# A graph network with sorted neighbours: due times step by step, the order of loads, and three small edits around TensorE

## The chip, the cores and the metric

The kernel runs on one core of a Trainium2 chip. The metric is device time in microseconds (us). Five engines of the core matter here: PE (TensorE, the matrix engine), PEld (its weight loads, which overlap with matmuls), DVE (VectorE), ACT (ScalarE) and POOL (GpSimd); SP issues most of the DMAs. Each engine executes its instructions in the order in which the program gives them, and waits at an instruction whose inputs aren't there.

## The reference

There are 128 graphs of N = 128 nodes with F = 64 features, and a dense matrix `adj` (128 x 128) for each, about 6% of it non-zero. Two layers follow one another, each with a residual and a layer norm:

```
mask = adj > 0
h  = relu(x_j @ W1a + (x_j - x_k) @ W1b + b1)          # for each pair j, k; H = 192
hm = sum over k of mask[j, k] * h[j, k]
x  = layernorm(x + hm @ W2 + deg[j] * b2)              # deg = row sums of mask
agg = adj @ x
x  = layernorm(x + elu(elu(agg @ V1 + c1) @ V2 + c2) @ V3 + c3)
```

## The kernel before, in words

**Tiling.** Two graphs make a pair (index s), and there are NP = 64 pairs p. For a node j, the sum over k needs only its neighbours. The kernel therefore counts the degrees, sorts the nodes of each graph by degree (a rank by comparisons, then a permutation matrix), and gives each of the 9 column blocks of sorted nodes (BLOCKS) a fixed number of neighbour slots. For a block of w nodes with s slots, n = s*w columns; the nine n make E = 1323 columns a graph. A one-hot matrix `oh` (from a running count of the mask along the sorted nodes) picks the neighbour for each slot by a matmul, so that the sum over k becomes a sum over slots.

**One pair, step by step** (line numbers of the kernel before):

- `prepare` (L502): mask and degrees on DVE (L511), keys on POOL (L518), `spread` on PE (L524 spreads the degrees over the columns; L526 makes a row 0, 1/128, ... from the constants `small` and `iotb`), `rank` on DVE (L533), `permute` on DVE (L541: permutation matrix `permb`, comparing L526's row in PSUM with the ranks).
- `sort_x` (L548): the sorted x (L556), then `project_a` (L564): three f32 matmuls L570 and the bias on ACT (L577) make `aj`; POOL and DVE make a correction for unused slots (L584, L596, L603), with a small matmul step L589/L591.
- `sort_mask` (L606): L612, L615 on PE, copies on ACT (L620, L622), a running count L626, then nine one-hot blocks on DVE (L636).
- `turn` (L645): transposes of adj and x (L651, L652), one copy on ACT (L656).
- `project_c` (L661): the neighbours' half of the first product, for each of the two graphs one f32 matmul with 64 rows of contraction and 256 columns (L669; graph 0 uses rows 0 to 63 of the array, graph 1 rows 64 to 127), and a bias row (L672). Its 256 columns are 192 of the hidden layer and 64 of the product with W2. The result is split into three bf16 parts on ACT, DVE and POOL (L679, L683, L686, L688): `cp`.
- nine `unit`s (L803): ACT copies `aj` into one of NE = 4 PSUM banks (L811), 18 bf16 matmuls add the neighbours' parts (`gather`, L823; columns 0 to 63 and 64 to 127 of the array work as two tiles), DVE reduces over the slots (L832) into `sums`.
- `finish` (L736): `hm` on POOL (L741); `project` on PE (L746 with `hm`, L750 with the sorted mask and `cp`, L753 counts the slots from a column of ones); `ys` on ACT (L757), a store of the counts (L759), `unsort` (L763), a norm (L691: DVE, POOL, ACT), `aggregate` (L770), two hidden layers (L778/L780 and L786/L787, each with exp on ACT and a DVE step), `last` (L792/L794), a second norm and the store of the result.

After the loop, `dense` computes pairs whose degrees don't fit the slots in another way. With these inputs it only finds that there are none.

**What sets the order.** The class `Flow` (L63) is a planner that runs when the program is built. Every pair has several threads (generators); each yields its next step as (engine, cost, events it needs, PSUM banks it needs, function). `Flow.run` keeps a clock for each engine, finds for each thread when its step could start, takes the engine with the earliest, and among the steps that could start within NEAR of that the one with the smallest due time (`_rank`). A step that would change TensorE's tiling mode (`PE` or `PE:t`) ranks HOLD later and costs SWITCH more. The function then emits the instructions. So costs and due times decide only the order on each engine; the chip runs it with semaphores. Before, a thread has one due time at its start and moves by a fixed pace with each step (STEP = 1.94, or 0.1 for constants); pair p's preparation begins when pair p - AHEAD's gathers do, with AHEAD = 3 and ROUND = 11.39 a pair. `load` (L496) issues the DMAs of adj and x on SP; the planner takes them as there 2.5 after its latest clock.

Of the kernel before, what the change touches and what calls it, by code (L numbers as in the profile page):

```python
# [87 lines left out]
class Flow:  # L88
# [10 lines left out]
    NEAR = 0.1  # L99
    NEAR_PE = 0.05  # L100
    SWITCH = 0.1
    HOLD = 5
# [8 lines left out]
    def start(self, due, pace, gen):  # L111

        self.serial += 1
        th = [due, self.serial, pace, gen, None]
        self._next(th, None)

    def _next(self, th, got):
        try:
            th[4] = th[3].send(got)
        except StopIteration:  # L120
            if th in self.threads:
                self.threads.remove(th)
            return
        if th not in self.threads:
            self.threads.append(th)
        elif got is not None:
            th[0] += th[2]
# [50 lines left out]
def sparse(tc, env):  # L178
# [6 lines left out]
    NE = 4  # L185
# [7 lines left out]
    ROUND = 11.39  # L193
    AHEAD = 3
    PACE = ROUND / NB
    STEP = 1.94
    TURN = 4
    CS = 3
    SORT = 5
    FIN = 0.5  # L200

    def due(p, step):
        return ROUND * (p - AHEAD) + STEP * step

    def pace(u):
        return PACE * u

# [26 lines left out]

    def fetch(t, src):
        nc.sync.dma_start(t, src)
# [24 lines left out]
    wc = const([P, H + O], F32, "wc")  # L261
# [9 lines left out]
    b2p = const([P, O], BF16, "b2p")  # L271
# [35 lines left out]
    def arrive_next():  # L307
        halves(nc.sync, b1c, g.b1, [[1, HB], [HB, 3]])
        fetch(b2r, bass.AP(tensor=g.b2.tensor, offset=g.b2.offset, ap=[[0, P], [1, O]]))
        happened([6.0], "const", "b1")  # L310
        happened([6.0], "const", "b2")

    def arrive_late():
        fetch(v2s, g.v2)
        fetch(v3s, g.v3)
        for s in range(2):
            fetch(v1d[s * F:(s + 1) * F], g.v1)
        for c, lo, times in ((g.c1, 0, 1), (g.c2, H1, 1), (g.c3, 2 * H1, 2)):
            n = c.shape[0]
            fetch(rows[:, lo:lo + times * n].rearrange("p (t n) -> p t n", t=times),  # L320
                  bass.AP(tensor=c.tensor, offset=c.offset, ap=[[0, P], [0, times], [1, n]]))
        happened([14.0], "const", "v")
        happened([14.0], "const", "c")
# [12 lines left out]
    def consts_pool():  # L336
# [11 lines left out]
        flow.start(0.1, 0.1, consts_prefix(below))  # L348
        yield from op("POOL", 0.2, lambda: v.memset(b2p, 0.0), "b2p0")
# [8 lines left out]
        yield from op("POOL", 1.0, scale, "srow")  # L358
        for s in range(2):
            yield from op("POOL", 0.3, lambda: v.memset(v1p[:, s], 0.0), f"v1p0{s}")  # L360
# [9 lines left out]
    def consts_dve():  # L370
# [8 lines left out]
        yield from op("DVE", 0.4, lambda: v.memset(wad, 0.0), "wad0")  # L379

# [14 lines left out]
    def consts_w():  # L395

        v = nc.vector
        yield from op("DVE", 0.25, lambda: v.tensor_scalar(wc[:, 0:H], w1s[:, 1], -1.0, None,
# [15 lines left out]
        ev, = yield ("DVE", 0.2, [ev], 0, lambda: v.tensor_scalar(wc[:, H:H + O], t[:, :O], 0.5,  # L414
# [13 lines left out]
    def consts_b2():  # L428
        last = ["b2", "b2p0"]
        for name, fn in parts(b2r, b2p, O):  # L430
            yield from op("POOL", 0.25, lambda: fn(nc.gpsimd), "b2" + name, *last)
            last = ["b2" + name]
        happened(event("const", "b22"), "const", "b2p")
# [68 lines left out]
    def prepare(p):  # L502
# [19 lines left out]
        def spread(key):  # L522
            for s in range(2):
                nc.tensor.matmul(key[:, s * N:(s + 1) * N], degb[:, s:s + 1].to_broadcast([P, P]),  # L524
                                 identb, start=True, stop=True)
            nc.tensor.matmul(key[:, 2 * N:3 * N], small, iotb, start=True, stop=True)  # L526
        ev, key = yield ("PE", 0.17, [ev] + made("identb", "small", "iotb"), 1, spread)
# [8 lines left out]
        ev, = yield ("DVE", 0.54, [ev] + made("tie"), 0, rank)  # L536
        permb = d["permb"] = prep.tile([P, 2, N], BF16, name="permb")

        def permute():
            for s in range(2):  # L540
                nc.vector.tensor_scalar(permb[:, s, :], key[:, 2 * N:3 * N], pos[:, s:s + 1], None,  # L541
                                        op0=OP.is_equal)
        ev, = yield ("DVE", 0.51, [ev], 0, permute)
        flow.give(key, ev)
        flow.start(due(p, SORT), STEP, sort_x(p, ev))
        flow.start(due(p, SORT), STEP, sort_mask(p, ev))
# [98 lines left out]
    def turn(p):  # L645
# [13 lines left out]
        flow.start(due(p, CS), STEP, project_c(p, ev))  # L659

    def project_c(p, ev):  # L661

        d = S[p]
        cols = H + O

        def project(*cps):
            for s in range(2):
                k = slice(s * F, (s + 1) * F)
                nc.tensor.matmul(cps[s][:, :cols], d["turned"][k, 2, :], wc[k, :],  # L669
                                 start=True, stop=False)  # L670
            for s in range(2):
                nc.tensor.matmul(cps[s][:, H:cols], onesb[:, :P], b2p, start=False, stop=True)  # L672
        ev, *cps = yield ("PE", 0.7, [ev] + made("wc", "b2p", "onesb"), 2, project)
# [62 lines left out]
    def finish(p):  # L736
# [5 lines left out]

        def project(yb):
            cp, mtp = d["cp"], d["mtp"]
            for c in range(3):
                nc.tensor.matmul(yb[:, :2 * O], hm[:, c, :], flat(w2d[:, c]),  # L746
                                 start=(c == 0), stop=False)
            for s in range(2):
                for i in range(3):
                    nc.tensor.matmul(yb[:, s * O:(s + 1) * O], mtp[:, s, :], cp[:, i, s, H:H + O],  # L750
                                     start=False, stop=(s == 1 and i == 2))
            for s in range(2):
                nc.tensor.matmul(yb[:, 2 * O + s:2 * O + s + 1], mtp[:, s, :], onesb[:, 0:1],  # L753
                                 start=True, stop=True)
        ev, yb = yield ("PE", 0.9, [ev] + made("w2d"), 1, project)
        ys = work.tile([P, 2 * O + 2], F32, name="ys")
        ev, = yield ("ACT", act(2 * O + 2), [ev], 0, lambda: nc.scalar.copy(ys, yb[:, :2 * O + 2]))  # L757
        flow.give(yb, ev)
        nc.sync.dma_start(g.degs[:, 2 * p:2 * p + 2], ys[:, 2 * O:])  # L759

        def unsort(t):
            for s in range(2):
                nc.tensor.matmul(t[:, s * O:(s + 1) * O], d["permT"][:, s, :],  # L763
                                 ys[:, s * O:(s + 1) * O], start=True, stop=True)
# [74 lines left out]
    def begin(p):  # L839
        if p < NP:  # L840
            load(p)
            happened([max(flow.clock.values(), default=1.0 + p) + 2.5], "load", p)
            flow.start(due(p, 0), STEP, prepare(p))
            flow.start(due(p, TURN), STEP, turn(p))
# [3 lines left out]
    def lane(u, ev):  # L848
        p = units[u][0]
        if p not in begun:  # L850
            begun.add(p)
            begin(p + AHEAD)
            flow.start(ROUND * (p + FIN), STEP, finish(p))
        ev = yield from unit(u, ev)
        if u + NE < len(units):
            flow.start(pace(u + NE), PACE, lane(u + NE, ev))

    nc.vector.memset(mone, -1.0)
    for p in range(min(AHEAD, NP)):
        begin(p)  # L860
        if p == 0:
            arrive_next()
    arrive_late()
    flow.start(-101.0, 0.1, arrive())
    flow.start(-100.0, 0.1, consts_pool())
    flow.start(-99.0, 0.1, consts_dve())
    flow.start(-98.0, 0.1, consts_w())
    flow.start(-97.0, 0.1, consts_wad())
    flow.start(-96.0, 0.1, consts_b2())
    flow.start(-95.0, 0.1, consts_banks())  # L870
    flow.start(ROUND * -0.5, 1.0, consts_late())
    for k in range(NE):
        flow.start(pace(k), PACE, lane(k, [0.0]))
# [217 lines left out]
```

## Time and profile before

| what | before |
|---|---|
| median of 3 runs | 788.52 us (788.28 to 788.82) |
| the profiled execution | 789.11 us |
| its span, first to last instruction | 787.3 us |
| granted TensorE clock, mean | 0.991 |
| PE busy | 756.4 us (96%), 14551 matmuls |
| PEld busy | 684.9 us (87%) |
| DVE busy | 736.8 us (94%) |
| ACT busy | 661.6 us (84%) |
| POOL busy | 441.7 us (56%) |
| costliest group: gather matmuls L823 | 376.4 us, 10368 of them |

A page of the profile gives the busy time of each engine, the span in slices, the DMA queues, the chain of work that ended last, and groups of instructions (line, engine, operation, out<-in, count, busy us, mean ns, idle before it and what ended it). Matmuls are pipelined and their ends are modelled, so that their durations overlap; what a matmul takes of TensorE's time is read from the distance between starts. A timeline lists instructions in order of time, with equal neighbours merged: start, length from the first start to the last end, count. f32 matmuls appear as two records each.

### The profile page before, as it was taken

The page shows a single profiled execution, that of the slowest core. Times are in us where ns is not written, and L with a number is a line of the kernel's source. Part 1 is how long each engine was busy: PE and PEld are TensorE (multiplying, and loading weights), DVE is VectorE, ACT ScalarE, POOL GpSimd, SP SyncE. Part 2 cuts the span into 40 slices and gives each one's busy share as a digit, 9 for nine tenths or more (in the row PEclk, how much of TensorE's full clock was granted, in tenths as well). Part 3 has the DMA queues.
Part 4 walks back from the last instruction along what each step waited for, and adds up shares of the span by engine and source line. Part 5 has one row for each costly group of instructions (what it writes and reads, how often), then busy time and mean ns, then how long its engine had stood idle before and what let it go on. Part 6 is the DMA issues. An engine that isn't in the chain of part 4 may idle for free.

```text
span 787.3 us, 35836 instructions
## 1 busy us (share of the span) xinstructions
PE 756.4 (96%) x14551; PEld 684.9 (87%) x14552; DVE 736.8 (94%) x2421; ACT 661.6 (84%) x1862; POOL 441.7 (56%) x806
## 2 busy tenths in 40 slices
PE   4889999999999999999999999999999999999994
PEld 2578999999999999999999999999999999999983
DVE  3899999999999999999999999999999999999982
ACT  1868889898989989898998989889898988989862
POOL 4445556555655655565565556556556655655542
PEclk9999999999999999999999999999999999999996
DMA  3000101101101110110111011011101101110000
GB/s 95 2 2 23 27 22 27 30 20 30 26 20 30 27 29 20 30 27 20 30 27 29 21 30 26 20 30 26 30 20 31 26 20 30 27 28 21 9 9 14
DMA packets 63884, 19.91 MB, mean 25 GB/s; under 512 B 46560, under 2 KB 63712, under 8 KB 63712
## 3 DMA queue, kind: packets, MB, share of 16 engines
q1 hardware_dynamic: 63008, 17.25, 9.4%
q8 instruction: 116, 1.90, 1.0%
q14 instruction: 56, 0.46, 0.2%
q10 hardware_dynamic: 704, 0.30, 0.1%
HBM read 13.27 MB, written 4.19 MB: 22 GB/s over the span
## 4 chain that ended last, share of the span: by engine, by line
PE 91%; DVE 4%; ACT 1%; DMA 1%; issue 1%; SPq 1%; POOL 1%; ACTq 0%; POOLq 0%; DVEq 0%
PE e L823 43%; PE m L570 6%; PE m L746 6%; PE m L669 5%; PE m L780 4%; PE m L794 4%; PE m L787 4%; PE m L763 4%; PE m L770 2%; PE m L556 2%; PE m L651 2%; PE m L750 1%; PE m L672 1%; PE m L589 1%; DVE sums L832 1%; DVE oh L636 1%
## 5 line engine op out<-in xcount | busy, mean ns | idle before, releaser
L823 PE MATMUL e<-oh,cp 128*64 128x162 bf16 (+3 forms) x10368 | 376.4, 228 | 5.4 <-ACT e L811 3.8
L823 PEld LDWEIGHTS <-cp 128*64 128x64 bf16 x10368 | 349.1, 110 | 24.4 <-issue 16.9
L832 DVE TENSOR_REDUCE sums<-e 128x54 f32<-128x486 f32 (+8 forms) x576 | 345.6, 610 | 4.2 <-PE e L823 1.9
L811 ACT COPY e<-aj 128x504 f32<-128x504 f32 (+6 forms) x576 | 300.2, 549 | 17.0 <-DVE sums L832 11.6
L636 DVE TENSOR_TENSOR oh<-vp,slotc 128x336 bf16<-128x336 bf16 (+6 forms) x576 | 168.3, 321 | 0.7 <-PE e L823 0.5
L688 POOL TENSOR_TENSOR cp<-r,cp 128x512 bf16<-128x512 f32 x64 | 74.8, 1170 | 73.8 <-ACT cp L686 73.7
L709 POOL TENSOR_TENSOR rs<-ve,mhalf 128x2 f32<-128x2 f32 x128 | 89.2, 697 | 10.6
L577 ACT ACTIVATE aj<-m,b1c 128x128 f32<-128x128 f32 x192 | 56.5, 365 | 34.7 <-PE m L570 34.6
L741 POOL TENSOR_TENSOR hm<-sums,corr 128x384 f32<-128x384 f32 x64 | 64.3, 1004 | 31.1 <-DVE sums L832 31.1
L518 POOL CAST degb<-deg 128x2 bf16<-128x2 f32 x64 | 12.4, 193 | 122.5 <-DVE mk L511 122.5
L584 POOL TENSOR_TENSOR sa<-aj,srow 128x384 f32<-128x384 f32 x64 | 64.1, 1001 | 15.6 <-ACT xsT L560 8.3
L603 POOL TENSOR_TENSOR corr<-ea,sa 128x384 f32<-128x384 f32 x64 | 64.0, 1001 | 11.2 <-DVE ea L596 11.2
L679 ACT CAST cp<-m 128x256 bf16<-128x256 f32 x128 | 41.6, 376 | 33.3 <-PE m L672 33.2
L729 ACT ACTIVATE e<-m,mone 128x256 f32<-128x256 f32 x128 | 60.7, 474 | 6.7 <-PE m L787 3.7
L708 POOL TENSOR_SCALAR ve<-st 128x2 f32<-128x2 f32 x128 | 24.5, 191 | 67.1 <-DVE st L701 61.6
L732 DVE SCALAR_TENSOR_TENSOR h<-e,m 128x256 f32<-128x256 f32 x128 | 53.0, 414 | 5.5 <-ACT e L729 5.5
L570 PE MATMUL m<-xsT,wad 128*128 128x128 f32 x384 | 57.6, 287 | 0.5 <-DVE h L732 0.5
L746 PE MATMUL m<-w2d,hm 128*128 128x128 f32 x384 | 54.3, 278 | 0.0
L683 DVE TENSOR_TENSOR r<-m,cp 128x256 f32<-128x256 f32 x128 | 48.5, 419 | 5.8
L719 ACT ACTIVATE x<-y,nb,rs 128x64 f32<-128x64 f32 x128 | 51.1, 464 | 0.9 <-POOL nb L712 0.8
L570 PEld LDWEIGHTS m<-xsT,wad 128*128 128x128 f32 x384 | 48.7, 194 | 0.9 <-DVE h L732 0.7
L746 PEld LDWEIGHTS m<-w2d,hm 128*128 128x128 f32 x384 | 48.0, 192 | 1.1 <-POOL hm L741 0.2
(147 smaller groups left out, 1416.6 us busy)
## 6 DMA issues: line engine op xcount, KB each, us to landing
adj<-in_adj_dram SPq DMA_DIRECT2D x64, 128.0 KB, 2.4
xx<-in_x_dram SPq DMA_DIRECT2D x64, 64.0 KB, 2.1
out_dram<-o SPq DMA_DIRECT2D x64, 64.0 KB, 1.6
degs<-ys SPq DMA_DIRECT2D x64, 1.0 KB, 1.6
w1s<-in_L_gnn_W_dram ACTq DMA_DIRECT2D x2, 96.0 KB, 3.1
rows<-in_L_gnn_b_dram SPq DMA_DIRECT2D x3, 64.0 KB, 3.4
w2s<-in_L_gnn_W_dram ACTq DMA_DIRECT2D x2, 48.0 KB, 2.7
v2s<-in_L_gnn_W_dram SPq DMA_DIRECT2D x1, 64.0 KB, 2.3
```

What stands on the lines that cost most here:

```text
L570: nc.tensor.matmul(aps[:, c * N:(c + 1) * N], wad[:, c, :], xsT, start=True, stop=True)
L584: evs, = yield ("POOL PORT", 0.95, [have] + made("srow"), 0, lambda: nc.gpsimd.tensor_mul(sa, aj, srow))
L603: ev, = yield ("POOL PORT", 1.05, [ev, evs], 0, lambda: nc.gpsimd.tensor_sub(corr, ea, sa))
L636: lambda: nc.vector.tensor_tensor(oh[:, :, c].rearrange("p b (s w) -> p b s w", w=w), vp[:, :, p0:p1].rearrange("p b (o w) -> p b o w", o= ...
L688: lambda: nc.gpsimd.tensor_sub(cp[:, 2], r1, cp[:, 1]))
L709: nc.gpsimd.tensor_tensor(rs, ve, mhalf, op=OP.pow)
L729: lambda: nc.scalar.activation(e, z, AF.Exp, bias=mone))
L741: lambda: nc.gpsimd.tensor_sub(hm, d["sums"], d["corr"]))
L746: nc.tensor.matmul(yb[:, :2 * O], hm[:, c, :], flat(w2d[:, c]), start=(c == 0), stop=False)
L811: lambda: nc.scalar.copy(e.rearrange("p (c s w) -> p c s w", c=3, w=w), d["aj"][:, :, p0:p1].rearrange("p c (o w) -> p c o w", o=1) .to_br ...
L823: nc.tensor.matmul(e[s * HB:(s + 1) * HB, c * n:(c + 1) * n], cp[:, k, s, c * HB:(c + 1) * HB], oh[:, s, base:base + n], start=False, stop ...
L832: nc.vector.tensor_reduce(d["sums"][:, :, p0:p1], e.rearrange("p (c s w) -> p c w s", c=3, w=w), AX.X, OP.add, apply_absolute_value=True)
```

## The change

- **Due times.** Every step gets a due time of its own, from a table DUE (relative to 10.83 times the pair's number), in place of start plus pace. NEAR goes from 0.1 to 0.05, HOLD from 5 to 1.3, ROUND from 11.39 to 10.83, AHEAD from 3 to 4. `consts_pool`, `consts_dve` and `consts_b2` are partly put off.
- **Queue of loads.** The planner keeps a clock of SP's queue (`queued`), and `arrive_late`, which loads the second net's weights, is called after the loads of the first five pairs.
- **Counts from a column of ones.** `wc` and `b2p` get two columns more; the bias row writes ones into them. `cp` is then 258 wide, and its W2 part has a column of ones on either side. The L750 matmuls take 65 columns and give the counts with the product; the L753 matmuls go. The L750 matmuls stand ahead of those with `hm`.
- **Row tiles of C in turns.** L669's two matmuls of 256 columns become four of 129: first half of graph 0, of graph 1, second half of graph 0, of graph 1.
- **Permutation from a row in SBUF.** `permute` compares with `iotb` in SBUF (bf16, the rank as it is), and L526 goes.

```diff
-    NEAR = 0.1
+    NEAR = 0.05
-    HOLD = 5
+    HOLD = 1.3
...
-    def start(self, due, pace, gen):
+    def start(self, base, due, gen):
...
+        th[0] = th[5] + next(th[3], th[0] - th[5])
         if th not in self.threads:
             self.threads.append(th)
-        elif got is not None:
-            th[0] += th[2]
...
-    ROUND = 11.39
-    AHEAD = 3
+    ROUND = 10.83
+    AHEAD = 4
     PACE = ROUND / NB
-    STEP = 1.94
-    TURN = 4
-    CS = 3
-    SORT = 5
-    FIN = 0.5
...
+    DUE = {
+        "prepare": (-44.8, -59.6, -54.3, -49.4, -45.1),
+        "sort_x": (-26.9, -23.7, -23.1, -22.6, -17, -21.2, -16.5, -16.5, -21.8),
+        "sort_mask": (-21.1, -43.6, -19.4, -7.5, -12.1, -5.1, -3, -0.9, 0.5, 0.1, 0.5, 6.9, 7,
+                      11.5),
+        "turn": (-44.7, -37.6),
+        "project_c": (-29.2, -26.7, -30.6, -30.3, -23.4, -20.3, -25.3),
+        "finish": (27.2, 19.6, 18.9, 24.1, 25.9, 27.6, 31.3, 28.1, 22.5, 34.7, 38.1, 42.8, 40.5,
+                   44, 46.5, 46.7, 52.9, 53, 54.5, 58.2, 65.2),
+        "unit": (1.7, 26, 7.9),
+    }
...
+    SP = [0.7]
+
+    def queued(cost):
+
+        SP[0] = max(SP[0], max(flow.clock.values(), default=0.0)) + cost
+        return [SP[0] + 2.6]
...
-    wc = const([P, H + O], F32, "wc")
+    wc = const([P, H + O + 2], F32, "wc")
-    b2p = const([P, O], BF16, "b2p")
+    b2p = const([P, O + 2], BF16, "b2p")
...
+        yield from op("POOL", 0.2, lambda: v.memset(b2p[0:1], 1.0), "b2p1")
...
-            nc.tensor.matmul(key[:, 2 * N:3 * N], small, iotb, start=True, stop=True)
-        ev, key = yield ("PE", 0.17, [ev] + made("identb", "small", "iotb"), 1, spread)
+        ev, key = yield ("PE", 0.11, [ev] + made("identb"), 1, spread)
...
         ev, = yield ("DVE", 0.54, [ev] + made("tie"), 0, rank)
+        flow.give(key, ev)
...
-                nc.vector.tensor_scalar(permb[:, s, :], key[:, 2 * N:3 * N], pos[:, s:s + 1], None,
+                nc.vector.tensor_scalar(permb[:, s, :], iotb, pos[:, s:s + 1], None,
                                         op0=OP.is_equal)
-        ev, = yield ("DVE", 0.51, [ev], 0, permute)
-        flow.give(key, ev)
+        ev, = yield ("DVE PORT", 0.24, [ev] + made("iotb"), 0, permute)
...
-            for s in range(2):
-                k = slice(s * F, (s + 1) * F)
-                nc.tensor.matmul(cps[s][:, :cols], d["turned"][k, 2, :], wc[k, :],
-                                 start=True, stop=False)
+            half = cols // 2
+            for c in range(2):
+                for s in range(2):
+                    k = slice(s * F, (s + 1) * F)
+                    nc.tensor.matmul(cps[s][:, c * half:(c + 1) * half], d["turned"][k, 2, :],
+                                     wc[k, c * half:(c + 1) * half], start=(c == 0), stop=False)
...
-        ev, *cps = yield ("PE", 0.7, [ev] + made("wc", "b2p", "onesb"), 2, project)
+        ev, *cps = yield ("PE", 0.6, [ev] + made("wc", "b2p", "onesb"), 2, project)
...
+            for s in range(2):
+                for i in range(3):
+                    nc.tensor.matmul(yb[:, s * (O + 1):(s + 1) * (O + 1)], mtp[:, s, :],
+                                     cp[:, i, s, H + 1 - s:H + 2 + O - s],
+                                     start=(s == 0 and i == 0), stop=False)
             for c in range(3):
-                nc.tensor.matmul(yb[:, :2 * O], hm[:, c, :], flat(w2d[:, c]),
-                                 start=(c == 0), stop=False)
-            for s in range(2):
-                for i in range(3):
-                    nc.tensor.matmul(yb[:, s * O:(s + 1) * O], mtp[:, s, :], cp[:, i, s, H:H + O],
-                                     start=False, stop=(s == 1 and i == 2))
-            for s in range(2):
-                nc.tensor.matmul(yb[:, 2 * O + s:2 * O + s + 1], mtp[:, s, :], onesb[:, 0:1],
-                                 start=True, stop=True)
-        ev, yb = yield ("PE", 0.9, [ev] + made("w2d"), 1, project)
+                nc.tensor.matmul(cut(yb), hm[:, c, :], w2d[:, c], start=False, stop=(c == 2))
+        ev, yb = yield ("PE", 0.8, [ev] + made("w2d"), 1, project)
...
-            happened([max(flow.clock.values(), default=1.0 + p) + 2.5], "load", p)
-            flow.start(due(p, 0), STEP, prepare(p))
-            flow.start(due(p, TURN), STEP, turn(p))
+            happened(queued(1.0), "load", p)
+            begin_thread("prepare", p, prepare(p))
+            begin_thread("turn", p, turn(p))
...
+    for k in range(NE):
+        flow.start(pace(k), DUE["unit"], lane(k, [0.0]))
     arrive_late()
...
     flow.run()
```

## The prediction

> **What bounds the kernel now.** I read the stages first (the busy time of each engine in stretches of the span), because a share over the whole span mixes a start, a steady part and an end. Columns: stretch, length, then busy us (instructions) of PE, PEld, DVE, ACT, POOL, clock, DMA share, GB/s.
> ```profile
> 0.00:40.00 40.00, 25.78 (x258) 17.85 (x261) 24.30 (x111) 19.92 (x58) 17.41 (x54) 1.00 0.19 48
> ...
> 200.00:300.00 100.00, 100.00 (x1996) 91.96 (x1995) 98.11 (x326) 88.74 (x253) 58.90 (x107) 1.00 0.11 27
> ...
> 750.00:787.30 37.30, 24.97 (x366) 20.48 (x365) 18.55 (x51) 16.14 (x42) 10.69 (x25) 0.80 0.06 12
> ```
> In the steady part TensorE has no idle time: PE bounds it, and DVE at 98% is close behind but late for nothing. All PE idle time is at the two ends, 14.2 and 12.3 us there and 30.9 us in all (787.3 - 756.4). The chain that ended last agrees: PE 91%. In the list of its pieces the same four gather units (72 matmuls, 2.53 us) return at 236.48 and 247.97, 282.45 and 293.94: one pair of graphs takes 11.49 us, 64 pairs 735 us, start and end some 52.
>
> So a round is a sum over PE, and what an instruction costs is the distance from its start to the next start, not its duration (those overlap). The PE timeline of one round gives it (start, length, line, count of passes; an f32 matmul is recorded as two passes):
> ```profile
> 402.46 0.70 PE L669 MATMUL m<-wc,turned 64*128 64x256 f32 x4
> 403.10 0.23 PE L672 MATMUL m<-b2p,onesb 128*128 128x64 bf16 x2
> ...
> 405.54 0.83 PE L746 MATMUL m<-w2d,hm 128*128 128x128 f32 x6
> 406.21 0.34 PE L750 MATMUL m<-cp,mtp 128*128 128x64 bf16 x6
> 406.39 0.19 PE L753 MATMUL m<-onesb,mtp 128*128 128x1 bf16 x2
> 406.44 0.22 PE L792 MATMUL m<-rowp,onesb 128*128 128x128 bf16 x1
> 406.50 0.61 PE L794 MATMUL m<-v3s,h 128*128 128x64 f32 x4
> 406.94 0.28 PE L524 MATMUL m<-identb,degb 128*128 128x128 bf16 x2
> 407.05 0.22 PE L526 MATMUL m<-iotb,small 128*128 128x128 bf16 x1
> 407.11 0.61 PE L763 MATMUL m<-ys,permT 128*128 128x64 f32 x4
> 407.56 0.89 PE L570 MATMUL m<-xsT,wad 128*128 128x128 f32 x6
> 408.28 0.27 PE L626 MATMUL m<-mtp,prefix 128*128 128x256 bf16 x1
> ```
> Read it by differences: L669 0.64, L746 0.67 (0.112 a pass), L750 0.18 (0.029 each), L753 0.05, L526 0.06, L794 and L763 0.44-0.45. L794 and L763 move 64 columns yet cost 0.112 a pass, as L746 does with 128[...].
>
> The start, PE and then the queue of loads (SPq):
> ```profile
> 8.71 0.42 PE L652 MATMUL m<-ident,xx 128*128 128x128 f32 x1
> 16.24 0.66 PE L651 MATMUL m<-ident,adj 128*128 128x128 f32 x2 [7.11 <-DMA adj<-in_adj_dram]
> 17.04 1.54 PE L411 MATMUL m<-w2s,sums 64*128 64x64 f32 x6
> 18.51 0.40 PE L524 MATMUL m<-identb,degb 128*128 128x128 bf16 x2
> ```
> ```profile
> 5.34 0.47 SPq L498 DMA_DIRECT2D adj<-in_adj_dram  x1
> ...
> 8.53 1.53 SPq L236 DMA_DIRECT2D rows<-in_L_gnn_b_dram  x3
> 10.11 0.47 SPq L498 DMA_DIRECT2D adj<-in_adj_dram  x1
> ```
> PE stands 7.11 us before the transposes of the fourth pair, whose load is issued at 10.11 behind seven loads of weights and rows and lands 6 us later. The rank matmuls L524 of the first pairs, ready long before, wait behind it.
>
> [...] L652 before the gather lasts 0.20 us to the next start where L651 lasts 0.109, so 0.09 a switch. [...] the nearest rows here are L541 (f32 from PSUM, 338 ns) and L377 (bf16 in SBUF, 214 ns).
>
> **The change, part by part** (order of the built kernels compared; us per round unless said).
> 1. *Permutation from a row.* The matmul L526 goes: -0.056. L541 reads iotb in SBUF: 2 x (338 - 214 ns) = 0.25 us of DVE a pair less, between 0 and 0.4. DVE is not late for anything in the steady part, so this is worth nothing there; it counts at the start, where DVE is full. Free on TensorE otherwise: the bank was held for it, and is now given back earlier.
> 2. *Counts from a column of ones.* The two L753 go: -0.055. The six L750 matmuls move 65 columns and not 64 (+0.003), and stand ahead of the three f32 matmuls with hm. Before, those followed L780, whose passes (0.112) hid the first weight load. Now the load hides behind one 0.029 pass: +0.083. Sum -0.055 + 0.003 + 0.083 = +0.031; from -0.05 (load hidden after all) to that. The ys copy and the one SP store of the counts keep their number and size.
> 3. *Row tiles of C in turns.* Four f32 matmuls of 129 columns for two of 256. Single records decide here: the first two passes of L669 start at 402.464 and 402.470 and last 480 ns, the next two at 402.784 and 402.790, 376 ns. So the two row tiles already run side by side[...]. In turns it is 0.104 + 4 x 0.112 + 0.1 = 0.652 for 0.632: +0.02. If half-length passes let a tile run ahead, at best one pass less: -0.1. I take +0.02, and 0.002 for L672's 66 columns. The extra columns cost ACT, DVE and POOL 1% of their cp steps; they have slack.
> 4. *Order by due times.* In both orders a steady round enters and leaves the tiled mode twice; over the kernel there are 276 switches for 272: +0.4 us once, HOLD or not. What changes is which pass stands before an f32 weight load. Before: L792-L794, L526-L763 and L763-L570 leave 0.056 open each, 0.167. After: last layer behind its constant row and project_a behind that, 0.112; the unsort now follows the 256-column passes of hidden2 (0.218) and pays nothing; the transposes behind the rank +0.005. Sum -0.167 + 0.112 + 0.005 = -0.051 (rounded).
> Steady, parts 1 to 4: -0.056 + 0.031 + 0.022 - 0.051 = -0.054, times 64: **-3.4 us**. Part 2 stands at its upper end, since nothing longer than 0.029 is there to hide the load.
> What is queued behind new places: ys on ACT stands after turned (0.50) and one bank copy (0.55); with its own 0.27 that is 1.3 us, and between project and unsort PE now has last, project_a, sort, hidden2: 0.5 + 0.73 + 0.22 + 0.55 = 2.0. From the last gather of a pair to project lie 5 us of PE work, 4.2 before. The longest run of gathers without a longer break is six tiles on four banks, eight before. All of that speaks for PE staying full.
> 5. *Queue of loads.* Five adj/xx pairs are now issued before the weights of the second net: the fourth adj goes out at about 6.4 (two issues of 0.5 after 5.34) and, at 3 to 4 us, lands about 10; SP, ACT and DMA do the same work in another order. On PE the rank of the first pair now stands before the second pair's transposes, so it waits no more for the fourth load. Late next: w2s and L411, the iotas of slotc and srow on POOL (until 6.4) ahead of the first degb, then about 7 to 9 us for the first rank (18.5 before). The rows of constants now land later, about 15, and are needed only by the first hidden layers. After that DVE is the limit until 55 (21.84 busy of 22.13 from 32.87), where PE still has 4.8 us idle; part 1 eases it by 0.25 x 6. Of the 7.1 us wait I count **6.5**; bounds 1 (DVE or POOL fills the gap) and 11 (first rank 9 us earlier, and DVE's relief).
> 6. *End.* After the last gather before, PE has 6.1 us of steps left, after 9.5 (17 blocks by the same prices), under a chain of 22.6 us with idle time (12.3 us). So up to 3.4 us of work moves under the tail; DVE may hold the last gathers (0.61 us each), and I count **-2**, from +1 to -3.4.
> Sum against the profiled execution (span 787.3, time 789.11): -3.4 + 0.4 - 6.5 - 2 = -11.5, which makes 777.6. The median of the runs is 0.6 below that execution: **777.0**.
>
> **The rivals.**
> A. *The start does not shorten* (wait replaced by DVE, POOL or w2s). For: DVE is full from 32.87 to 55. Against: DVE stood idle 6.34 us at 16.13 on the same load. Gain 3.4 - 0.4 + 1 = 4: 784.5.
> B. *TensorE saves more*: row tiles at -0.1 and the load hidden in part 2, so -0.12 and -0.08 more a round, or about 0.15 of that 0.2: 9.6 us more, 767.4. [...] Against: the 6 ns between the records of L669.
> C. *Slower*: unsort waits for ys. ACT is 89% busy and in order; ahead of turned stands the cp cast (0.64), which waits for DVE. If DVE is late with r there, ys is late, PE stands before unsort, and project_a, prefix and the next gathers stand behind. It decides once ys comes more than 2.0 us after project, and turns the sum once that excess passes 11.5/64 = 0.18. At 0.35 a round: +22 - 11.5 = 799. Against: DVE falls from 98% to 96%.
> D. *The turns or the column do nothing or cost*: in the sum already (+0.02, +0.03).
>
> **How the numbers follow.** Forecast 0.56, A 0.20, B 0.17, C 0.07. Within 0.2% (1.6 us, about what measurement can tell from no change) lies only the far end of A, 0.03. So faster 0.90, same 0.03, slower 0.07. The range leaves out C and the far part of B: 766 to 786.
>
> **What would show it.** Right: PE 100% in the steady stretches with a round of 11.44; L696's four matmuls 0.65 to the next start; 0.11 between the last bf16 product and the first with hm; no wait near 7 us on adj at the start, first gather at 23 to 27 (32.87 before); DVE about 96%. Wrong: a round below 11.35 (B), PE idle in the middle before unsort (C), or first gathers past 30 (A). The weakest step is the start, a wait exchanged for others that this profile cannot order.

## The result, and the profile after

| what | before | after |
|---|---|---|
| median | 788.67 us (788.28 to 788.97) | **839.11 us** (838.04 to 840.18) |
| ratio, 95% interval | | 1.064 [1.0621, 1.0659] |
| span of the profiled execution | 787.3 | 838.0 |
| one round (a pair), between the 15th and the 55th | 11.493 | 12.615 |
| first gather | 32.87 | 20.98 |

The change is 6.4% slower, where 1.5% faster was predicted. The start is 12 us shorter, more than forecast; the round is 1.12 us longer, and there are 64 of them.

The stages after, columns as in the prediction (stretch, length, busy us of PE, PEld, DVE, ACT, POOL, clock, DMA share, GB/s):
```profile
0.00:40.00 40.00, 32.45 (x380) 26.23 (x382) 31.82 (x135) 25.71 (x76) 23.55 (x62) 0.91 0.19 49
200.00:300.00 100.00, 94.80 (x1801) 85.30 (x1803) 99.17 (x295) 82.19 (x230) 57.16 (x96) 1.00 0.10 23
...
800.00:838.00 38.00, 27.04 (x462) 23.63 (x456) 22.28 (x61) 19.92 (x53) 13.77 (x31) 0.89 0.08 16
```
PE had no idle time in the steady part and now has 5%; DVE went from 98 to 99%. That it does so with fewer instructions (295 for 326 in 100 us, about 37 a round in both) is the first hint: DVE isn't doing more, its instructions last longer. The chain that ended last says the same. PE was 91% of it:
```profile
PE 49%; DVE 36%; ACT 5%; POOL 5%; issue 2%; DMA 0%; ACTq 0%; DVEq 0%; POOLq 0%
```
The groups on the page show which instructions: the one-hots and the permutes (mean ns of one before: 321 and 338).
```profile
L660 DVE TENSOR_TENSOR oh<-vp,slotc 128x336 bf16<-128x336 bf16 (+6 forms) x576 | 215.7, 402 | 2.4 <-PE e L851 2.3
...
L566 DVE TENSOR_SCALAR permb<-iotb,pos 128x128 bf16<-128x128 bf16 x128 | 73.0, 610 | 0.0
```
Means hide the form of it, the DVE timeline shows it (start, length from the first start to the last end, count):
```profile
401.40 1.29 DVE L660 TENSOR_TENSOR oh<-vp,slotc 128x338 bf16<-128x338 bf16 x2
...
406.09 0.33 DVE L660 TENSOR_TENSOR oh<-vp,slotc 128x336 bf16<-128x336 bf16 x1
406.34 1.31 DVE L566 TENSOR_SCALAR permb<-iotb,pos 128x128 bf16<-128x128 bf16 x2
```
and beside it POOL's timeline of the same stretch:
```profile
401.57 1.02 POOL L768 TENSOR_TENSOR hm<-sums,corr 128x384 f32<-128x384 f32 x1 [1.21 <-DVE sums L860]
...
406.09 1.35 POOL L715 TENSOR_TENSOR cp<-r,cp 128x516 bf16<-128x516 f32 x1 [0.54 <-ACT cp L713]
```
Two one-hots take 0.49 us elsewhere and 1.29 here; they end when POOL's `hm` has ended (402.59). Two permutes take 1.31, and the first ends with POOL's third part of `cp` (407.44). In 40 rounds, one permute of the two lasts about 1147 ns beside L715 in 39 of them (the other 241), and one one-hot about 1035 ns beside L768 in all 40. The wait isn't idle time in the profile: it stands inside the instruction's duration, so that DVE looks busy.

In the trace of before, between 200 and 700 us, no one-hot and no permute is above 348 ns. Outside that stretch five one-hots are, of 551 to 1240 ns, each beside a wide POOL step. So the sign stood in the profile of before, at its start (DVE, then POOL; the first of the two POOL steps ends at 33.49, the one-hot at 33.69):
```profile
32.52 1.17 DVE L636 TENSOR_TENSOR oh<-vp,slotc 128x336 bf16<-128x336 bf16 x1
```
```profile
32.20 2.50 POOL L688 TENSOR_TENSOR cp<-r,cp 128x512 bf16<-128x512 f32 x2 [2.75 <-ACT cp L686]
```

Per round, the nine one-hots take 3.62 us for 2.84 before, and the two permutes 1.37 for the 0.49 that they take undisturbed (kernel 10 below): 1.66 us of waits. DVE had 0.22 us idle a round, and the shorter permutes give 0.19. A DVE so full has no room for 1.66.

That gives **theory W**: waits of DVE on POOL make the round. In the steady part of the trace of after, the long one-hots beside `hm` start with 0.92 to 0.93 us of it left and end 107 to 112 ns after it; the long permutes beside `cp` start with 1.09 to 1.10 us of L715 left and end 49 to 55 ns after it. What in the chip holds them isn't shown by the profile. The runs below bear W out for POOL's wide steps, for its memsets with the plain permute alone, and not for its small steps (last section). Rivals: PE's own new order and its shorter runs of gathers (PE does wait 0.6 us a round before L650, on ACT), and wrong prices of the edits on PE.

### The profile page after: what moved, and what is told of

It is laid out like the page before. It is cut to its first block, busy times and chain, and to the rows that moved or that the text cites. A ratio compares the mean times of both kernels' runs of the same rounds, so it can differ in the third digit from the quotient of the medians.

```text
span 838.0 us, 35915 instructions
## 1 busy us (share of the span) xinstructions
PE 779.6 (93%) x14615; PEld 699.3 (83%) x14616; DVE 806.8 (96%) x2422; ACT 671.1 (80%) x1862; POOL 465.1 (56%) x807
## 4 chain that ended last, share of the span: by engine, by line
PE 49%; DVE 36%; ACT 5%; POOL 5%; issue 2%; DMA 0%; ACTq 0%; DVEq 0%; POOLq 0%
PE e L851 31%; DVE sums L860 11%; DVE permb L566 8%; DVE oh L660 6%; POOL corr L627 5%; ACT aj L601 4%; DVE cmp L557 4%; PE m L696 4%; PE m L798 3%; PE m L808 3%; PE m L650 2%; PE m L580 2%; DVE st L728 1%; DVE y L723 1%; DVE r L710 1%
## 5 line engine op out<-in xcount | busy, mean ns | idle before, releaser
L851 PE MATMUL e<-oh,cp 128*64 128x66 bf16 (+4 forms) x10368 | 385.2, 229 | 4.8 <-DVE oh L660 4.7
L839 ACT COPY e<-aj 128x504 f32<-128x504 f32 (+6 forms) x576 | 316.2, 561 | 56.6 <-DVE sums L860 54.6
L660 DVE TENSOR_TENSOR oh<-vp,slotc 128x336 bf16<-128x336 bf16 (+6 forms) x576 | 215.7, 402 | 2.4 <-PE e L851 2.3
L735 POOL TENSOR_SCALAR ve<-st 128x2 f32<-128x2 f32 x128 | 36.8, 287 | 129.4 <-DVE st L728 124.3
L768 POOL TENSOR_TENSOR hm<-sums,corr 128x384 f32<-128x384 f32 x64 | 65.2, 1019 | 77.7 <-DVE sums L860 77.6
L715 POOL TENSOR_TENSOR cp<-r,cp 128x516 bf16<-128x516 f32 x64 | 84.6, 1322 | 38.8 <-ACT cp L713 38.8
L627 POOL TENSOR_TENSOR corr<-ea,sa 128x384 f32<-128x384 f32 x64 | 65.8, 1028 | 30.5 <-PE m L798 25.5
L566 DVE TENSOR_SCALAR permb<-iotb,pos 128x128 bf16<-128x128 bf16 x128 | 73.0, 610 | 0.0
L608 POOL TENSOR_TENSOR sa<-aj,srow 128x384 f32<-128x384 f32 x64 | 64.3, 1004 | 3.9 <-ACT aj L601 3.8
L713 ACT CAST cp<-r 128x516 bf16<-128x516 f32 x64 | 39.8, 622 | 32.5 <-DVE r L710 32.5
L782 PE MATMUL m<-w2d,hm 128*128 128x128 f32 x384 | 58.3, 288 | 0.0
L601 ACT ACTIVATE aj<-m,b1c 128x128 f32<-128x128 f32 x192 | 56.2, 363 | 1.3 <-PE m L594 1.2
L576 ACT CAST permf<-permb 128x256 f32<-128x256 bf16 x64 | 26.0, 407 | 34.7 <-DVE permb L566 34.7
L710 DVE TENSOR_TENSOR r<-m,cp 128x258 f32<-128x258 f32 x128 | 52.6, 413 | 0.8 <-ACT cp L706 0.7
L746 ACT ACTIVATE x<-y,nb,rs 128x64 f32<-128x64 f32 x128 | 51.7, 473 | 0.5 <-DVE y L723 0.5
L650 PE MATMUL m<-mtp,prefix 128*128 128x256 bf16 x64 | 17.4, 271 | 35.3 <-ACT aj L601 34.7
```

The lines of the kernel that those rows point to most:

```text
L566: nc.vector.tensor_scalar(permb[:, s, :], iotb, pos[:, s:s + 1], None, op0=OP.is_equal)
L601: nc.scalar.activation(aj[:, c, :], aps[:, c * N:(c + 1) * N], AF.Identity, bias=b1c[:, c:c + 1])
L608: evs, = yield ("POOL PORT", 0.95, [have] + made("srow"), 0, lambda: nc.gpsimd.tensor_mul(sa, aj, srow))
L627: ev, = yield ("POOL PORT", 1.05, [ev, evs], 0, lambda: nc.gpsimd.tensor_sub(corr, ea, sa))
L660: lambda: nc.vector.tensor_tensor(oh[:, :, c].rearrange("p b (s w) -> p b s w", w=w), vp[:, :, p0:p1].rearrange("p b (o w) -> p b o w", o= ...
L715: lambda: nc.gpsimd.tensor_sub(cp[:, 2], r1, cp[:, 1]))
```

## The experiments

Every kernel keeps the whole computation unless its expectation says what it leaves out. Of each edit the main lines are shown, `...` for the rest. "Order of after" or "of before" means that the planner wasn't told of the edit, so that each engine's instructions stay in place. Times are medians, beside runs of before on the same chip (789.4 to 790.4).

**1. The permute with a sum beside it.** Order of after.
```diff
-                nc.vector.tensor_scalar(permb[:, s, :], iotb, pos[:, s:s + 1], None,
-                                        op0=OP.is_equal)
+                nc.vector.tensor_scalar(permb[:, s, :], iotb, pos[:, s:s + 1], 0.0,
+                                        op0=OP.is_equal, op1=OP.add,
+                                        accum_out=ones[:, s:s + 1])
```


> The changed kernel with the same order on every engine; only permute also writes its accumulator (the form of the mask count, L536, which takes 0.20 us an instruction and never lasted over 0.28). Theory W (permute and the one-hot products wait for whole POOL operations): permute loses its wait of 0.9 us a round, two of them take 0.40 in place of 1.23, the one-hots keep theirs of 0.7, DVE stays the bound, the round falls from 12.60 to about 11.8 and the time to about 787. Rival O (the due times leave steps too little distance, DVE is only where it shows): within 1% of 839. Rival S (the compare from SBUF is slow in itself): the time falls as under W, but the one-hot products keep single instructions over 1 us only if POOL matters, which S denies.

803.05 us, ratio 1.0167 [1.0145, 1.0188]; round 11.964. The permutes meet the same POOL instruction (108 of them start with 0.83 to 1.13 us of it left) and no longer wait:
```profile
L567 DVE TENSOR_SCALAR_CACHE_REDUCE permb<-iotb,pos 128x128 bf16<-128x128 bf16 x128 | 38.2, 333 | 0.0
```
So 36 of the 50 us lost hang on the form of one small instruction. One-hots still meet `hm` in 40 of 40 rounds (about 1.04 us). The expected total was too low, since I had counted more for the permute than it gave.

**2. The same, and `hm` held back on POOL** by a read of the last sums.
```diff
+        def subtract():
+            nc.gpsimd.tensor_copy(look, d["sums"][:, 0, BLOCKS[-1][0]:BLOCKS[-1][0] + 2])
+            nc.gpsimd.tensor_sub(hm, d["sums"], d["corr"])
...
-                     lambda: nc.gpsimd.tensor_sub(hm, d["sums"], d["corr"]))
+                     subtract)
```


> As e1_accum_permute, and POOL reads two columns of the last sums (0.19 us) ahead of hm, so that the one-hot product that DVE issues at the same moment comes first. Theory W: the one-hots' waits of 0.7 us a round go as well, DVE needs about 11.1, TensorE is the bound again at my sum of 11.44, and the time is about 839 - 64 x 1.16 = 765. Rival O: no gain over e1. If hm's delay only moves the collision to another POOL operation: between 765 and 787.

813.46 us, 1.030 [1.0282, 1.0317]; round 12.149: slower than 1, a miss. The meeting with `hm` is gone, and in 38 of 40 rounds a one-hot now meets the third part of `cp` (up to 1101 ns). Moving one POOL step moves the meeting. DVE's total isn't what makes this round: its one-hots last less in sum than in kernel 1 (3.34 us for 3.65), and DVE is idle 0.51 us a round. The one-hot that is held here stands just ahead of the permutes, and TensorE stands 0.5 us a round before L652, the running count; the section on why follows that path.

**3. `hm` on DVE, so that POOL has one step less to meet.** Kernel 1 with this edit:
```diff
-                     lambda: nc.gpsimd.tensor_sub(hm, d["sums"], d["corr"]))
+                     lambda: nc.vector.tensor_sub(hm, d["sums"], d["corr"]))
```


> The changed kernel in its order, with the permute that sums beside it, and with the subtraction that makes hm on DVE in place of POOL (about 0.45 us of DVE a round). It takes away the one POOL operation that a one-hot still met in each round (wait 0.7 us) and keeps the others. If that wait was the rest of the loss: DVE -0.7 + 0.45, PE the bound again, round 11.6 to 11.7, 776 to 783 (803.1 with hm on POOL). Rival: as with the late hm, the one-hots slide into the third part of cp instead: one of them about 1.1 us in each round, round 12.0 to 12.2, 803 to 815.

835.85 us, 1.0585 [1.0566, 1.0603]; round 12.607. The rival holds, beyond its size: the one-hots meet `cp` in 40 of 40 rounds. Its DVE timeline:
```profile
401.95 1.33 DVE L662 TENSOR_TENSOR oh<-vp,slotc 128x336 bf16<-128x336 bf16 x1
...
411.13 0.55 DVE L770 TENSOR_TENSOR hm<-sums,corr 128x384 f32<-128x384 f32 x1
```
and POOL's, where the third part of `cp` starts 0.04 us ahead of that one-hot:
```profile
401.91 1.17 POOL L717 TENSOR_TENSOR cp<-r,cp 128x516 bf16<-128x516 f32 x1 [0.53 <-ACT cp L715]
```
In the changed kernel (above) both started at 406.09; there the one-hot kept its 0.33 and POOL took 1.35 in place of 1.17. Some tens of ns decide who waits: POOL for 0.18, with 43% of its time idle, or DVE for 1.0, with under 1% (both in the changed kernel).

**4. POOL without wide reads.** Kernel 1 with POOL's four wide steps (L608, L627, L715, L768) replaced, so that they take place but read almost nothing (what they compute is left out):
```diff
+    def stand(to, of):
+        look = work.tile([P, 2], F32, name="look", bufs=12)
+        nc.gpsimd.tensor_copy(look, of)
+        for k in range(2):
+            nc.gpsimd.memset(to, 0.0)
...
-                     lambda: nc.gpsimd.tensor_sub(hm, d["sums"], d["corr"]))
+                     lambda: stand(hm, d["sums"][:, 0, BLOCKS[-1][0]:BLOCKS[-1][0] + 2]))
```


> As e1_accum_permute (order of the changed kernel), and POOL's four wide operations a pair (sa, corr, hm, third part of cp) read only two columns each and write zeros twice; so the third part of cp, the correction and hm are left out, with their places, waits and readers kept. Theory W: no DVE instruction has to wait, DVE falls to about 11.0, TensorE is the bound, the round is my sum 11.44 and the time about 765. Rival O (the due times leave too little distance): little changes against e1, about 800. If POOL's writing alone also holds DVE: as e1.

778.13 us, 0.9851 [0.9836, 0.9867]; round 11.631, PE 99.9% busy; 765 was expected, and kernel 5 finds most of the difference. POOL is as busy as before, and between 200 and 700 us no one-hot is above 347 ns. This decides for W against the rival of PE's order: the order of the changed kernel, freed of these waits, has PE full.

**5. The same with the plain permute.**
```diff
-                nc.vector.tensor_scalar(permb[:, s, :], iotb, pos[:, s:s + 1], 0.0,
-                                        op0=OP.is_equal, op1=OP.add,
-                                        accum_out=ones[:, s:s + 1])
+                nc.vector.tensor_scalar(permb[:, s, :], iotb, pos[:, s:s + 1], None,
+                                        op0=OP.is_equal)
```


> The order of the changed kernel and its plain permute (no sum beside it), with POOL's four wide steps made of a read of two columns and two memsets each (it leaves out the third part of cp, the correction of unused slots and their difference hm, which are zero). Against the run with the sum beside the permute, 778.1 with no long instruction on DVE. If POOL must read two wide inputs to hold DVE: permute about 245 ns, no instruction over 0.6 us, 777 to 779. Rival: the plain permute is held by POOL's writing alone, though the one-hots are not: one permute a round 0.6 to 1.2 us as in the changed kernel (1147 ns), 785 to 800.

768.72 us, 0.9723 [0.9707, 0.974]; round **11.451**, PE 100%. Neither expectation gave that time, though the second one's mechanism shows. DVE's timeline, then POOL's:
```profile
405.09 0.34 DVE L666 TENSOR_TENSOR oh<-vp,slotc 128x336 bf16<-128x336 bf16 x1
405.35 0.55 DVE L572 TENSOR_SCALAR permb<-iotb,pos 128x128 bf16<-128x128 bf16 x2
```
```profile
404.70 1.11 POOL L525 MEMSET cp<- 128x516 bf16 x2
```
The one-hot runs through beside a memset; the two permutes end together, 445 ns each on average for 245 undisturbed, when the second of the two memsets, which began just ahead of them, ends. So here a POOL instruction that only writes holds the plain permute and not the one-hot. It costs little, since a memset lasts 0.53 us. And the sum beside the permute in kernel 4 (about 340 ns, and 78 ns to read it out) wasn't free: PE stands 0.18 a round longer before the running count there, the whole difference of the two rounds.

**6. POOL's wide steps in pieces**, whole computation, plain permute, order of after.
```diff
-                     lambda: nc.gpsimd.tensor_sub(cp[:, 2], r1, cp[:, 1]))
+                     lambda: pieces(nc.gpsimd.tensor_sub, cp[:, 2], r1, cp[:, 1]))
```
These are four pieces of 129 columns; `hm`, `sa` and `corr` go in three of 128.

> The changed kernel, whole, in its order, with POOL's four wide steps issued in pieces: 128 columns three times for hm, the correction and its product, 129 columns four times for the third part of cp. The work is the same. If DVE is held for one POOL instruction at a time and gets its turn between two of them, a meeting costs at most a piece (estimated 0.45 us: 1.02 us for 384 columns, 0.195 for 2) and not the 0.9 and 0.7 us of the changed kernel. DVE then loses some 0.5 us a round in place of 1.6, POOL grows by some 1.7 us to about 8.8 of 11.6, PE becomes the bound again: round 11.5 to 11.7, 772 to 785; I say 778, which would be below both kernels. Rival: DVE does not get in between two pieces, or each following one-hot meets the next piece, so that the sum of the waits stays: round 12.2 to 12.7, 815 to 845.

793.82 us, 1.0049 [1.0035, 1.0063]; round 11.860. The stretch from 400 to 500:
```profile
400.00:500.00 100.00, 98.08 (x1960) 91.28 (x1956) 98.09 (x313) 88.63 (x246) 70.23 (x178) 1.00 0.10 25
```
Same work, same order, POOL 14 points busier, and 0.755 of the 1.12 us are back: DVE is held for one POOL instruction at a time and gets in between two (a piece of `cp` lasts 454 ns on average, a permute 442). The permutes wait 0.2 each, the one-hots 0.28 a round in all. 16 us more than I said are left, and it doesn't beat the kernel before. The round is 0.41 longer than kernel 5's, and by the distances between starts all of it stands on PE before the running count (0.80 us from unsort to count for 0.39 there).

**7. The planner with truer costs.** It keeps a clock called PORT, in the kernel before too: the one-hots, POOL's wide steps and now the permute share it, and in its plan they never overlap.
```diff
-    ev, = yield ("DVE PORT", 0.24, [ev] + made("iotb"), 0, permute)
+    ev, = yield ("DVE PORT", 0.4, [ev] + made("iotb"), 0, permute)
...
-    ev, *cps = yield ("PE", 0.6, [ev] + made("wc", "b2p", "onesb"), 2, project)
+    ev, *cps = yield ("PE", 0.66, [ev] + made("wc", "b2p", "onesb"), 2, project)
...
-    ev, yb = yield ("PE", 0.8, [ev] + made("w2d"), 1, project)
+    ev, yb = yield ("PE", 0.93, [ev] + made("w2d"), 1, project)
```


> The changed kernel, whole, with three costs of the planner set to what the trace shows: C 0.66 for 0.60, project 0.93 for 0.80, permute 0.40 for 0.24. Nothing that is computed changes, only the order. The planner keeps a clock called PORT which the permutes, the one-hots and POOL's wide operations share, so in its own plan they never overlap; they meet on the chip because the plan's times are not the chip's. If wrong costs are why they meet, truer ones take most of the meetings away: no permute or one-hot over 0.6 us, round about 11.6, 775 to 785. Rival: the plan lacks waits, weight loads and issue times altogether, three costs do not cure that, and the order is dealt anew into other meetings: long one-hots or permutes in most rounds, round 11.9 to 12.6, 800 to 845. I hold the rival a little likelier (805), after two runs in which another order made other meetings.

825.42 us, 1.0444 [1.0427, 1.0462]; round 12.296. Between the two: the permute meets `cp` in 20 of 40 rounds and not in 39, the one-hots still meet `hm` in all. The plan orders each engine by itself, and no event of the program makes POOL wait for DVE's turn.

**8 and 9. Parts alone, the planner told.** Part 1 alone (the row in SBUF), then parts 2 and 3 alone (counts, turns), on the kernel before with its due times, and the diff's own costs.

> The kernel before with only the permutation from a row in SBUF (L526 gone, the planner told so). Theory W: it depends on where permute and POOL meet in that order; without a meeting -0.056 x 64 = -3.6, so 785; with one instruction of each pair waiting for a POOL operation of 1 us up to +0.9 - 0.25 us of DVE a round, DVE at 11.9 and about 815. Single permutes are then either about 0.24 or over 1 us. Rival S: every permute near 0.6 us, DVE 11.8, about 808 wherever it stands.

839.65 us, 1.0636 [1.0618, 1.0653]; round 12.43 on average. A miss: its permutes hardly wait (249 ns on average, the longest 364), but the order was dealt anew and is irregular, with 326 changes of TensorE's mode (two column tiles or not) for 274 in before, and 23 one-hots above 0.6 us in 40 rounds, beside all four of POOL's wide steps.

> The kernel before with only the counts from a column of ones and the row tiles in turns. By my prices: -0.055 + 0.003 + 0.083 for the counts, +0.022 for the turns, so +0.05 us a round and about 792. If the turns save one pass of four and the weight load is hidden (rival B of the prediction): -0.1 - 0.05, so about 778.

845.52 us, 1.0715 [1.0697, 1.0733]; round 12.622. A miss of the same kind: these parts leave the permute as it was and add only two columns to `cp`'s steps, yet a one-hot meets the third part of `cp` in 40 of 40 rounds. So these two can't price parts. They show that the order of before happens to have no such meeting in its steady part; each of the other four that the planner made here (the changed kernel, 7, 8 and 9) has some.

**10 to 12. Parts alone in the order of before.** Kernel 10 is part 1, and the second net's weights loaded after the fourth pair:
```diff
-            nc.tensor.matmul(key[:, 2 * N:3 * N], small, iotb, start=True, stop=True)
...
-                nc.vector.tensor_scalar(permb[:, s, :], key[:, 2 * N:3 * N], pos[:, s:s + 1], None,
+                nc.vector.tensor_scalar(permb[:, s, :], iotb, pos[:, s:s + 1], None,
...
-    arrive_late()
...
+    arrive_late()
```


> The kernel before with the permutation from a row in SBUF and the fourth pair's loads ahead of the second net's weights, the planner not told, so that every engine but SP keeps its order. Theory W: permute meets only the short rs step of POOL there, so no wait; -0.056 x 64 = -3.6 for the matmuls and about -6 at the start: about 779. If permute waits for rs (0.7 us): DVE +0.5 a round, about 11.6, and 785 to 790. Rival S (slow form): permute near 0.6 us, DVE 11.8, about 800.

**781.43 us, 0.9897 [0.9881, 0.9912]**: below both kernels. Round 11.476, PE 100% from 400 to 500, first gather 26.24 for 32.87. Its permutes:
```profile
L540 DVE TENSOR_SCALAR permb<-iotb,pos 128x128 bf16<-128x128 bf16 x128 | 26.6, 253 | 0.0
```
The same instruction as in the changed kernel, at 253 ns for 610. In the 40 steady rounds all 80 run beside POOL's power step (L708, on 128x2), and none is above 255 ns: the row in SBUF is harmless where no wide POOL step runs beside it.

Kernel 11 is part 2 alone (columns of ones, L750's matmuls first, L753 gone):

> The kernel before with only the counts from a column of ones, the planner not told, so that the order is that of before. My price: -0.055 + 0.003 + 0.083 = +0.031 a round, +2, so about 791. Rival B of the prediction (load hidden): -0.05 a round, about 785. If a wait of DVE on POOL comes up (cp's third part is wider): well over 791, with one-hots over 1 us in the trace.

791.64 us, 1.0026 [1.0016, 1.0036]; round 11.539, +0.046.

Kernel 12 is part 3 alone (four matmuls of 128 columns):

> The kernel before with only the row tiles in turns (four matmuls of 128 columns for two of 256), the order else that of before. My price: +0.016 to +0.022 a round, so +1 and about 790. Rival B: one pass of four saved, -0.1 a round, about 782.

790.32 us, 1.0012 [1.0005, 1.0018]; round 11.505, +0.012.

## Why the prediction was wrong, step by step

**The step that failed is the DVE half of part 1**: "2 x (338 - 214 ns) = 0.25 us of DVE a pair less, between 0 and 0.4". Measured: 0.69 us more (1.37 for 0.68). The bounds came from two rows of durations, neither of which holds a wait; that of L377 is a single instruction at 1.8 us. What the edit changes is not only the speed of the instruction but whether a wide POOL step holds it. From PSUM it wasn't held (in kernel 9 seven permutes from PSUM start with 0.6 to 0.9 us of a wide POOL step left, and last 333 to 344 ns); from SBUF in its plain form it was (1147 ns beside L715), and with a sum beside it not (333 ns, kernel 1). The diff itself said it: the permute goes from "DVE" to "DVE PORT". I printed that line and priced only the instruction.

**"DVE is not late for anything ... DVE falls from 98% to 96%"** failed with it. At 98% busy, DVE had 0.22 us a round to give, and no wait on it could be bounded at nothing. Kernel 5, with 0.4 us of such waits a round left, shows 95.3%.

**Part 4, "All of that speaks for PE staying full"**, failed on the second half of the loss. I compared the two orders on PE and on ACT, but not DVE's one-hots against POOL's steps. The order of before kept them apart: between 200 and 700 us not one of its 393 one-hots overlaps one of POOL's four wide steps (1.0 to 1.2 us each); in the new order one meets `hm` in each round and is held, and one starts together with L715 and holds it for 0.2. Kernel 1 takes away the permute's share and leaves this one: 803.05, against 778.13 (kernel 4) with neither.

**How a wait on DVE reaches TensorE** was missing from part 4 too; I had followed only `ys`. Between 200 and 700 us the changed kernel's trace has these waits, among others (engine, line, releaser: us in all, times, longest):
```profile
PEld L851 <- issue: 36.8, 39, 0.9
...
PE m L650 <- ACT aj L601: 25.0, 40, 0.6
ACT permf L576 <- DVE permb L566: 24.5, 40, 0.7
...
PEld m L791 <- DVE y L723: 10.9, 40, 0.4
```
ACT's copy L576 waits for the held permute in every round. Behind it in ACT's order stand a bank copy and the bias step L601, and the count L650 waits, by the profile, for L601 (the first line is the same stand on the weight loads). From the start of unsort to the start of the count TensorE takes 0.39 us a round in kernel 5, 0.57 in 4, 0.65 in 1, 0.80 in 6, 1.09 in 2 and 1.28 in the changed kernel. In kernels 2, 4 and 6 this is all by which their rounds exceed kernel 5's; in the changed kernel it is 0.89 of 1.16, and 0.20 more stand in the gathers. The place belongs to the new order, but in that order it costs nothing once DVE is hardly held (kernel 5, PE 100%). So where a wait stands matters beside how long it is: kernel 2 has less of it in sum than kernel 1, ahead of the permute, and a longer round.

**Prices on PE held.** The sum for parts 1 to 4 was -0.054 a round; kernel 5 has -0.042 (11.451 for a predicted 11.44). Singly: turns +0.012 for +0.022; counts +0.046 for +0.031; the row -0.017 for -0.056. L526's 0.056 is gone in kernel 10, but by the distances between starts its gathers take 5.53 us a round for 5.49, which is the other 0.04; why they do is open. That the pass ahead counts is measured in the steady rounds: the first f32 pass takes 188 to 191 ns to the next start behind a 29 ns pass (L778 to L782, after), 164 or 165 behind one of 64 columns (L763 to L570, before), and 111 to 113 behind one of 128 (L780 to L746, before). The other two of part 4's three places show no such gap (L794's first pass 109, L763's 112), so their 0.056 is my estimate from the 0.112 and 0.056 between starts; so are the 0.104 (480 - 376 ns) and the 0.1 (what is left of 0.632) of part 3. By subtraction the order gives -0.083 for -0.051, which no run shows alone. In the changed kernel L696 takes 0.65 to the next start, as forecast:
```profile
401.19 0.72 PE L696 MATMUL m<-wc,turned 64*128 64x129 f32 x8
401.84 0.24 PE L699 MATMUL m<-b2p,onesb 128*128 128x66 bf16 x2
```

**Part 5 was right in mechanism, and priced too small.** PE doesn't wait for the fourth `adj` any more; the first ranks stand ahead of the transposes:
```profile
8.90 0.40 PE L549 MATMUL m<-identb,degb 128*128 128x128 bf16 x2
9.09 0.64 PE L675 MATMUL m<-ident,adj 128*128 128x128 f32 x2
...
20.98 1.11 PE L851 MATMUL e<-oh,cp 128*64 128x162 bf16 x36
```
If the steady rounds are run back from the 15th pair to the first, they begin at 37.0 before, 31.0 in kernel 10, 24.2 after, 23.2 in kernel 5. The loads (with the row) give 6.0, for my 6.5; the other 7 are left, by subtraction, for the new due times and the constants put off, which I hadn't priced and no run shows alone. (I had put all of PE's idle time of before at the two ends; 26.5 of the 30.9 us are there, and 4.2 lie between 40 and 100 us.) **Part 6** was too small as well: what is left for the end in kernel 5 is 3.9 us less (forecast 2, bound 3.4).

So the difference of the spans splits, in kernel 5 (766.9 - 787.3 = -20.4), into 64 x -0.042 = -2.7, start -13.8 and end -3.9; in the changed kernel (838.0 - 787.3 = +50.7) into start -12.8, 64 x 1.122 = +71.8 and end -8.3 (its last rounds meet less). The end is what is left over, so these sums test nothing. Run back by the first gathers and not, as here, by the first sums on DVE, kernel 5's start is -12.2 and its end -5.5.

**Rivals.** A (start doesn't shorten): refuted, kernel 10; its 784.5 also left out the 2 us of the end. B (TensorE saves more): refuted by 11 and 12. C had the right sign by another mechanism: unsort's weight loads (L791 above) wait up to 0.4 us, but for DVE's `y`, not for ys. The case that happened, DVE held by POOL, wasn't among my rivals. A 7% chance for slower was too low for a change that deals the order of five engines anew.

## What to carry to other kernels

Before an operand is moved from PSUM to SBUF, ask what runs on POOL beside the instruction: here the permute lasted 333 to 344 ns from PSUM beside a wide POOL step, and from SBUF 1147 in its plain form and 333 with a sum beside it. On a DVE that is nearly full (98% here), price each meeting at the remaining length of the wide POOL instruction (here 0.7 to 0.9 us), not at the instruction's own saving. Then ask what stands behind the held instruction in the orders of the other engines. A long-lasting instruction among equal short ones may be a wait, though the profile counts it as busy: compare the longest with the median over the whole trace, its two ends too, and look at the other engine at the moment it ends. An order without a meeting was worth more here than some hundredths on PE: make an edit in the old order first, and only then let a planner deal again; if meetings remain, shorter POOL instructions limit what each can cost (kernel 6: 0.2 us a permute for 0.9).

## What the runs showed that I had not expected

- POOL's small steps hold neither kind. In kernel 9, 78 one-hots start with 0.25 to 0.51 us of the power step (128x2, 0.70 us, inputs in SBUF) left, and last 332 to 341 ns; in kernel 8, 12 plain permutes start with 0.17 to 0.54 us of it left, and last 229 to 247 ns. Not every POOL instruction holds DVE, then; what it is about the wide ones that does wasn't tried.
- The wait goes in both directions, at small cost to POOL: 1.35 us for 1.17 where a one-hot came first.
- Splitting a POOL step of 1.02 us in three gave 1.30 in all, and one of 1.17 in four gave 1.69, its waits for DVE with it: 0.14 us a further piece in the first case.
- Taking POOL's step away (kernel 3) made the kernel 33 us slower than leaving it there (kernel 1): the meeting that replaced it was longer, and DVE got 0.55 us more work.
